# Two-layer relational graph convolution: sums by relation kept in a circle of 1024 nodes and projected once per block

## The chip, the cores and the metric

The kernel runs on one core of a Trainium2 chip. The metric is the device time of one execution in microseconds; the median of three runs before the change is 3974.79 us (3973.82 to 3981.2). A profile is one further execution, taken by the hardware profiler.

## The reference

Two layers of a relational graph convolution, then a residual and a layer normalisation. There are N = 12500 nodes of C = 128 features and E = 200000 edges, sorted by their target node `dst`. The type of an edge is the largest of ten of its attributes. Cut to what matters:

```python
def _rgcn_layer(x, src, dst, edge_type, w_rel, root, bias):
    seg = dst * NUM_REL + edge_type                       # NUM_REL = 10
    sums = segment_sum(x[src], seg, N * NUM_REL)
    cnt = segment_sum(ones, seg, N * NUM_REL)
    mean = (sums / maximum(cnt, 1)[:, None]).reshape(N, NUM_REL, -1)
    return einsum('nrd,rdo->no', mean, w_rel) + x @ root + bias

h = relu(_rgcn_layer(x, ..., w_rel1, root1, b1))
out = layernorm(x + _rgcn_layer(h, ..., w_rel2, root2, b2))
```

## The kernel before

**Tiles and groups.** The edges are cut into 1563 tiles of 128; one tile reaches over at most WN = 12 target nodes. Sixteen tiles are a group (97 full groups, then one of 8 and one of 3). Each layer runs over all groups in `layer` (L518).

**One group.** `gather` (L443) issues one indirect DMA per tile on POOL, which fetches the 128 source rows of the tile into `g`; three such buffers form a ring (RING = 3). `sums` (L454) builds on DVE one weighted one-hot matrix per tile, 128 edges by 120 columns (10 relations by 12 nodes), `oh` (L461), and TensorE multiplies `g` by it into `zp` in PSUM (L468). The first matmul in each group's order waits for all its gathers. An fp32 matmul shows as two records in the profile. ScalarE copies `zp` to `zs` (L482) in four pieces. `project` (L487) multiplies by the ten relation weights, two halves of 8 tiles, 40 records (L494), and ScalarE copies the result to `ms` (L500). `add` (L505) spreads the messages of the tiles over a window of 160 nodes with a further one-hot `at` (L465, L510), and DVE adds the window to the accumulator `acc`, 128 features by all nodes (L516), at an offset loaded into a register from the edges' first node (`bt`, L512, four offsets per load). Three groups are in flight: `sums` of k, `project` of k-1, `add` of k-2.

**Blocks.** When the groups that can touch a block of nodes are done (`done_after`, L76), the block is finished: 23 blocks of 512 nodes, then five of 128 and one of 84. `block_in` (L373) loads the block's own rows and transposes them on TensorE, `block_rows` (L391) adds the bias to the block's part of `acc` (L395), clears that part in layer 0 (L397), multiplies by `root` (L400) and brings the accumulator in by a product with the identity (L401). `hidden` (L408) applies ReLU and stores rows to `hD` in DRAM; `final` (L417) adds the residual, normalises on DVE and stores the output. Layer 1 gathers from `hD`, so its first gather waits for the last store of layer 0.

**What runs beside.** In layer 0 the types and counts of the edges are worked out for chunks of 128 tiles (`types`, `count`), spread over the groups as steps; they use DVE, PE and SP. Before the loop, `places` (L241) prepares the offsets, the first two chunks are typed and the first is counted. POOL does nothing in the loop but issue gathers. SP issues the loads and stores of blocks (L371).

**Order.** The order of instructions on each engine is chosen when the kernel is compiled, from dependences and the order of the program text; each engine then executes its queue in order. `tc.keep_in_program_order` and manual dependences pin a few of them. An instruction of DVE that uses a result of DVE waits for it. A general path for edges that do not fit the windows stands behind `tc.If(flag > 0)` (L738); it is not taken for this input.

Of the kernel before, what the change touches and what calls it, by code (L numbers as in the profile page):

```python
# [9 lines left out]
F32 = mybir.dt.float32  # L10
# [10 lines left out]
P = 128  # L21
# [3 lines left out]
WN = 12  # L25
# [4 lines left out]
HR = HT * WN  # L30
SW = 160
# [4 lines left out]
YB = 512  # L36
W = 128
# [6 lines left out]
def rgcn_resnorm_kernel(ctx: ExitStack, tc: tile.TileContext, x, src, dst, attr, w_rel1, root1, b1,  # L44
# [26 lines left out]
    NPAD = N + SW  # L71
# [15 lines left out]
    assert C == P and E % GT == 0 and 0 < HALF < P and NT % CT and groups[-1][1] > 1  # L87
# [5 lines left out]
    ps_f = ctx.enter_context(tc.tile_pool(name="ps_f", bufs=2, space=PSUM))  # L93
    ps_c = ctx.enter_context(tc.tile_pool(name="ps_c", bufs=1, space=PSUM))

    hD = dram.tile([N, C], F32, name="hD")
    KD = dram.tile([1, L + NT * P + L], F32, name="KD")
# [8 lines left out]
    zpool = fast.enter_context(tc.tile_pool(name="zpool", bufs=2))  # L106
    spool = fast.enter_context(tc.tile_pool(name="spool", bufs=3))
    ps_z = fast.enter_context(tc.tile_pool(name="ps_z", bufs=1, space=PSUM))
    ps_o = fast.enter_context(tc.tile_pool(name="ps_o", bufs=1, space=PSUM))
# [47 lines left out]
    def sources(c):  # L157
# [8 lines left out]

    columns = const.tile([P, SW], F32, name="columns")
    nc.gpsimd.iota(columns, pattern=[[1, SW]], base=0, channel_multiplier=0,
                   allow_small_or_imprecise_dtypes=True)
    iota = columns[:, :W]  # L170
    pads = const.tile([P, L + 1], I32, name="pads")
    nc.gpsimd.iota(pads, pattern=[[1, L + 1]], base=FAR, channel_multiplier=0)

    rank = const.tile([G, 2 * HR], F32, name="rank")
    nc.gpsimd.memset(rank, 1.0)
    nc.gpsimd.affine_select(rank, rank, pattern=[[1, 2 * HR]], compare_op=ALU.is_ge, fill=0.0, base=0,
                            channel_multiplier=-WN)
    nc.gpsimd.affine_select(rank, rank, pattern=[[-1, 2 * HR]], compare_op=ALU.is_ge, fill=0.0, base=WN - 1,
                            channel_multiplier=WN)
    lead = const.tile([G, 2 * HR], F32, name="lead")  # L180
    nc.gpsimd.memset(lead, 1.0)
    nc.gpsimd.affine_select(lead, lead, pattern=[[0, 2 * HR]], compare_op=ALU.is_equal, fill=0.0, base=0,
                            channel_multiplier=1)
    which = const.tile([G, 1], F32, name="which")
    nc.gpsimd.iota(which, pattern=[[0, 1]], base=0, channel_multiplier=WN, allow_small_or_imprecise_dtypes=True)
    row = const.tile([HR, 1], F32, name="row")
    nc.gpsimd.iota(row, pattern=[[0, 1]], base=0, channel_multiplier=1, allow_small_or_imprecise_dtypes=True)
    lane = const.tile([P, P], F32, name="lane")
    nc.gpsimd.iota(lane, pattern=[[1, P]], base=0, channel_multiplier=P,
                   allow_small_or_imprecise_dtypes=True)  # L190
    riota = const.tile([P, NREL], F32, name="riota")
# [3 lines left out]
    iotaP = bank[:, :SW]  # L195
    riotaP = bank[:, SW:SW + NREL]
# [13 lines left out]
    within = const.tile([HR, 1], F32, name="within")  # L210
    pw = ps_f.tile([P, YB], F32, name="pf")
    nc.tensor.matmul(pw[:HR, 0:1], rank[:, :HR], which, start=True, stop=True)
    nc.vector.tensor_tensor(within, row, pw[:HR, 0:1], op=ALU.subtract)
    nc.vector.tensor_tensor(rank, rank, lead, op=ALU.subtract)
    fl = const.tile([P, 1], F32, name="fl")
    nc.vector.memset(fl, 0.0)
    acc = const.tile([P, NPAD], F32, name="acc")
    negs = const.tile([1, L], F32, name="negs")
# [5 lines left out]
    bt = keep.tile([1, NG], I32, name="bt")  # L224
    b8_i = keep.tile([G, NG], I32, name="b8_i")
    full = NT // G
    nc.vector.memset(b8_i[:, full:], 0)
    nc.scalar.dma_start(bt[:, :full + 1], bass.AP(dst.tensor, dst.offset, [[1, 1], [G * P, full + 1]]))
    nc.scalar.dma_start(b8_i[:, :full], bass.AP(dst.tensor, dst.offset, [[P, G], [G * P, full]]))
    for k, (t, n) in list(enumerate(groups))[full:]:  # L230
        if k > full:
            nc.scalar.dma_start(bt[:, k:k + 1], bass.AP(dst.tensor, dst.offset + t * P, [[1, 1], [1, 1]]))
        m = n if t + n < NT else n - 1
        nc.scalar.dma_start(b8_i[:m, k:k + 1], bass.AP(dst.tensor, dst.offset + t * P, [[P, m], [1, 1]]))
    nc.scalar.dma_start(b8_i[m:n, NG - 1:], bass.AP(dst.tensor, dst.offset + E - P, [[1, 1], [1, 1]]))
    b8 = keep.tile([G, NG], F32, name="b8")
    place = keep.tile([HR, 2, NG], F32, name="place")
    wide = const.tile([P, 1], F32, name="wide")
    nc.vector.memset(wide, 0.0)

    def places():  # L241
        early(0, nc.vector.tensor_scalar(bt, bt, 0, N - 1, op0=ALU.max, op1=ALU.min))
        early(0, nc.vector.tensor_copy(b8, b8_i))
        pw = ps_f.tile([P, YB], F32, name="pf")
        for h in range(2):
            nc.tensor.matmul(pw[:HR, h * NG:(h + 1) * NG], rank[:, h * HR:(h + 1) * HR], b8, start=True, stop=True)
        nc.vector.tensor_scalar(place, pw[:HR, :2 * NG].rearrange("p (h g) -> p h g", h=2), within, None, op0=ALU.add)
        nc.vector.tensor_reduce(wide[:HR], place, axis=AX.XY, op=ALU.max)
# [123 lines left out]

    def block_in(k, l):  # L373

        n0, n, subs = block(k)
        last = "e" if k == NBLK - 1 else ""
        b = len(subs) if last else 4
        xb = fin.tile([P, b, C], F32, name="xb" + last)
        rows_dma(xb, x, k, False)
        fb = xb  # L380
        if l:
            fb = fin.tile([P, b, C], F32, name="hb" + last)
            rows_dma(fb, hD, k, False)
        pt = ps_f.tile([P, YB], F32, name="pf")
        for t, h in subs:
            nc.tensor.transpose(pt[:, t * P:t * P + h], fb[:h, t, :], ident[:h, :h])  # L386
        fT = fin.tile([P, b * P], F32, name="fT" + last)
        nc.scalar.activation(fT[:, :n], pt[:, :n], AF.Copy)  # L388
        return xb, fT

    def block_rows(fT, k, l):  # L391

        n0, n, subs = block(k)
        a = fin.tile([P, YB], F32, name="a")
        nc.vector.tensor_scalar(a[:, :n], acc[:, n0:n0 + n], bsb[l], None, op0=ALU.add)  # L395
        if l == 0:
            nc.vector.memset(acc[:, n0:n0 + n], 0.0)  # L397
        pr = ps_f.tile([P, 4, C], F32, name="pf")
        for t, h in subs:
            nc.tensor.matmul(pr[:h, t, :], fT[:, t * P:t * P + h], rsb[l], start=True, stop=False)  # L400
            nc.tensor.matmul(pr[:h, t, :], a[:, t * P:t * P + h], ident, start=False, stop=True)  # L401
        return pr
# [5 lines left out]
    def hidden(k, ready):  # L408

        xb, fT = ready  # L410
        pr = block_rows(fT, k, 0)
        hb = fin.tile([P, 4, C], F32, name="hb")
        for p, s in spans(k):
            nc.scalar.activation(hb[:p, s], pr[:p, s], AF.Relu)
        rows_dma(hb, hD, k, True)

    def final(k, ready):  # L417

        xb, fT = ready
        pr = block_rows(fT, k, 1)  # L420
# [30 lines left out]
    def halves(n):  # L451
        return [(h, min(HT, n - h * HT)) for h in range(-(-n // HT))]

    def sums(table, k, end):  # L454
# [8 lines left out]
        at = spool.tile([HR, 2, SW], F32, name="at")  # L463
        for h, _ in halves(n):
            nc.vector.tensor_scalar(at[:, h, :], iotaP[:HR], place[:, h, k:k + 1], None, op0=ALU.is_equal)  # L465
        zp = ps_z.tile([P, G // QB, YB], F32, name="zp")
        for j in range(n) if end else reversed(range(n)):
            m = nc.tensor.matmul(zp[:, j // QB, j % QB * KW:(j % QB + 1) * KW], g[:, j, :], oh[:, j, :],  # L468
                                 start=True, stop=True)
# [9 lines left out]
        zs = zpool.tile([P, NREL, G, WN], F32, name="zs")  # L479
        for b in range(-(-n // QB)):  # L480
            m = min(QB, n - b * QB)
            then("ACT", nc.scalar.activation(  # L482
                zs[:, :, b * QB:b * QB + m, :],
                zp[:, b, :m * KW].rearrange("c (j r n) -> c r j n", r=NREL, n=WN), AF.Copy))
        return k, zs, at

    def project(l, k, zs, at):  # L487

        n = groups[k][1]
        po = ps_o.tile([P, 2, C], F32, name="pp")  # L490
        ms = spool.tile([HR, 2, C], F32, name="ms")
        for h, m in halves(n):
            for r in range(NREL):
                nc.tensor.matmul(po[:m * WN, h], zs[:, r, h * HT:h * HT + m].rearrange("c j n -> c (j n)"),  # L494
                                 wsb[l][:, r, :], start=(r == 0), stop=(r == NREL - 1))
        if n % HT:
            for h, m in halves(n):
                nc.scalar.activation(ms[:m * WN, h], po[:m * WN, h], AF.Copy)
        else:
            nc.scalar.activation(ms[:, :n // HT], po[:HR, :n // HT], AF.Copy)  # L500
        return k, ms, at

    offs = []

    def add(k, ms, at):  # L505

# [266 lines left out]
```

## Time and profile before

| what | before |
|---|---|
| median of three runs | 3974.79 us |
| the profiled execution's own time | 4772.34 us |
| its span, first to last instruction | 4770.4 us |
| granted TensorE clock, mean | 0.739 |
| busy: PE / DVE / ACT / POOL | 2759.5 / 1511.5 / 527.0 / 2955.2 us |
| instructions: PE / DVE / ACT / POOL | 16162 / 4652 / 1136 / 3142 |
| DMA engines, mean busy share by slice | 0.1 to 0.4 |

The profiled execution took 798 us longer than the median of the runs. A line of the list of groups has line number, engine, operation, tiles, shapes and count, then busy time and the mean in ns of one, then the idle time of the engine just before, and what ended it; "issue" is time for which the profile shows no cause, and "remote" is a release that it could not trace. A line of the waits has engine, line and what it waited for, then the total, the number of waits and the longest. A line of the timeline has start, duration, engine, line, operation, tiles, shape and count, and in brackets the idle time before it. The chain of work that ended last is given by engine as:

```
another core or an unknown queue 34%; PE 33%; issue 21%; DVE 11%; ACT 1%; DMA 0%; DVEq 0%; ACTq 0%; SPq 0%
```

### The profile page before, as it was taken

Reading aid. Unit: us, or ns where it says so; the run is one execution under the profiler, and the core shown is the slowest. Engines: PE = TensorE matmul, PEld = TensorE weight load, DVE = VectorE, ACT = ScalarE, POOL = GpSimd, SP = SyncE. Lnnn points to the kernel's source line nnn. Section 1 sums busy time; section 2 is a strip of 40 time slices with the busy share of each in tenths; the row PEclk is TensorE's granted clock in tenths of the full one; section 3 lists DMA queues with packets and bytes.
Section 4 is the critical chain, followed back from the end, with each engine's and each line's share of the span. In section 5 each row is a group of like instructions: output and inputs, shape, how many; then the busy total and the mean of one; then the engine's idle time right before and its main releaser. Section 6 shows DMA issues by size and latency. Waiting matters only on the chain.

```text
span 4770.4 us, 43637 instructions
## 1 busy us (share of the span) xinstructions
PE 2759.5 (58%) x16162; PEld 2520.6 (53%) x16162; DVE 1511.5 (32%) x4652; ACT 527.0 (11%) x1136; POOL 2955.2 (62%) x3142
## 2 busy tenths in 40 slices
PE   2455556555655555666645555666655656565656
PEld 1455555555554545555544555555555555555556
DVE  5233333333333333333222222222222223222323
ACT  1011111111111101111110111111111111111111
POOL 5666665666656666666546666666666666666663
PEclk9677777777777777777776777777777777777778
DMA  4122122122221221212111211221222222222211
GB/s 141 44 79 74 50 74 74 50 75 62 61 77 47 75 62 51 57 48 52 46 49 46 54 52 51 53 56 51 52 56 53 52 52 58 51 52 52 58 52 40
DMA packets 180554, 279.00 MB, mean 58 GB/s; under 512 B 55623, under 2 KB 127190, under 8 KB 177206
## 3 DMA queue, kind: packets, MB, share of 16 engines
q0 software_dynamic: 100032, 205.07, 16.9%
q1 hardware_dynamic: 75428, 69.58, 4.6%
q8 instruction: 132, 2.16, 0.2%
q10 hardware_dynamic: 4872, 1.45, 0.1%
q14 instruction: 90, 0.74, 0.1%
HBM read 262.28 MB, written 13.60 MB: 58 GB/s over the span
## 4 chain that ended last, share of the span: by engine, by line
another core or an unknown queue 34%; PE 33%; issue 21%; DVE 11%; ACT 1%; DMA 0%; DVEq 0%; ACTq 0%; SPq 0%
PE pp L494 16%; PE zp L468 11%; DVE oh L461 7%; PE pp L510 2%; PE pf L401 1%; PE pf L400 1%; DVE at L465 1%; ACT zs L482 1%; DVE acc L516 1%; PE pf L343 0%; PE pf L345 0%; PE pf L386 0%; DVE o L436 0%; DVE st L429 0%
## 5 line engine op out<-in xcount | busy, mean ns | idle before, releaser
L445 POOL DMA_INDIRECT g<-in_x_dram,idxE x1563 | 1475.9, 944 | 911.2 <-issue 445.8
L445 POOL DMA_INDIRECT g<-hD,idxE x1563 | 1476.6, 945 | 865.3 <-issue 455.6
L494 PE MATMUL pp<-w,zs 128*96 128x128 f32 x7840 | 1358.2, 336 | 860.4 <-issue 722.1
L494 PEld LDWEIGHTS pp<-w,zs 128*96 128x96 f32 x7840 | 1232.0, 212 | 982.9 <-issue 834.6
L461 DVE TENSOR_SCALAR oh<-bank,keyE,wE 128x120 f32<-128x120 f32 x3126 | 1000.1, 400 | 644.6 <-remote 576.6
L468 PE MATMUL zp<-oh,g 128*128 128x120 f32 x6252 | 1033.5, 325 | 293.5 <-issue 259.9
L468 PEld LDWEIGHTS zp<-oh,g 128*128 128x128 f32 x6252 | 983.1, 240 | 314.0 <-issue 292.5
L482 ACT ACTIVATE zs<-zp 128x480 f32<-128x480 f32 (+1 forms) x782 | 382.9, 575 | 2167.7 <-remote 1912.9
L516 DVE TENSOR_TENSOR acc<-acc,pp 128x160 f32 x198 | 63.7, 322 | 1634.4 <-remote 1043.0
L510 PE MATMUL pp<-at,ms 96*128 96x160 f32 (+1 forms) x784 | 198.1, 386 | 591.1 <-issue 405.0
L510 PEld LDWEIGHTS pp<-at,ms 96*128 96x128 f32 (+1 forms) x784 | 142.5, 232 | 633.8 <-issue 437.1
L500 ACT ACTIVATE ms<-pp 96x256 f32<-96x256 f32 x196 | 74.1, 378 | 1241.3 <-remote 861.3
L341 DVE TENSOR_TENSOR eqb<-pf,kh 128x1344 bf16<-128x1344 f32 (+1 forms) x65 | 100.6, 1552 | 181.4 <-PE pf L345 82.3
L400 PE MATMUL pf<-root,fT 128*128 128x128 f32 x388 | 110.1, 379 | 79.0 <-issue 49.1
L401 PE MATMUL pf<-ident,a 128*128 128x128 f32 x392 | 114.0, 388 | 60.3 <-DVE a L395 22.0
L400 PEld LDWEIGHTS pf<-root,fT 128*128 128x128 f32 x388 | 87.0, 276 | 91.2 <-issue 55.8
L465 DVE TENSOR_SCALAR at<-bank,place 96x160 f32<-96x160 f32 x392 | 131.9, 376 | 0.0
L401 PEld LDWEIGHTS pf<-ident,a 128*128 128x128 f32 x392 | 90.7, 285 | 68.6 <-issue 24.6
L426 DVE TENSOR_TENSOR v<-pf,xb 128x512 f32<-128x512 f32 (+1 forms) x28 | 17.4, 620 | 243.2 <-remote 238.3
L348 DVE TENSOR_REDUCE wp<-pf 128x128 f32<-128x512 f32 (+1 forms) x13 | 9.0, 691 | 182.9 <-remote 175.5
L343 PE MATMUL pf<-eqb,identb 128*128 128x512 bf16 (+1 forms) x130 | 50.5, 388 | 17.9 <-DVE f L320 17.0
L388 ACT ACTIVATE fT<-pf 128x512 f32<-128x512 f32 (+1 forms) x56 | 30.2, 539 | 207.1 <-remote 151.3
(107 smaller groups left out, 483.0 us busy)
## 6 DMA issues: line engine op xcount, KB each, us to landing
m<-in_edge_attr_dram SPq DMA_DIRECT2D x24, 1344.0 KB
g<-in_x_dram,idxE POOLq DMA_INDIRECT x1563
g<-hD,idxE POOLq DMA_INDIRECT x1563
xb<-in_x_dram SPq DMA_DIRECT2D x46, 256.0 KB
hD<-hb SPq DMA_DIRECT2D x23, 256.0 KB
hb<-hD SPq DMA_DIRECT2D x23, 256.0 KB
out_dram<-o SPq DMA_DIRECT2D x23, 256.0 KB
w<-in_L_gnn_w_rel_dram ACTq DMA_DIRECT2D x2, 640.0 KB
```

Source lines behind the costliest of these rows:

```text
L341: nc.vector.tensor_tensor(eq[:p], kp[:p, None, :R].to_broadcast([p, DB, R]), ahead, op=ALU.is_equal)
L400: nc.tensor.matmul(pr[:h, t, :], fT[:, t * P:t * P + h], rsb[l], start=True, stop=False)
L401: nc.tensor.matmul(pr[:h, t, :], a[:, t * P:t * P + h], ident, start=False, stop=True)
L445: return g, [then("POOL", nc.gpsimd.indirect_dma_start(out=g[:, j, :], out_offset=None, in_=table, in_offset=bass.IndirectOffsetOnAxis(ap= ...
L461: then("DVE", nc.vector.tensor_scalar(oh[:, j, :], iotaP[:, :KW], keyE[:, t:t + 1], wE[:, t:t + 1], op0=ALU.is_equal, op1=ALU.mult))
L465: nc.vector.tensor_scalar(at[:, h, :], iotaP[:HR], place[:, h, k:k + 1], None, op0=ALU.is_equal)
L468: m = nc.tensor.matmul(zp[:, j // QB, j % QB * KW:(j % QB + 1) * KW], g[:, j, :], oh[:, j, :], start=True, stop=True)
L482: then("ACT", nc.scalar.activation(zs[:, :, b * QB:b * QB + m, :], zp[:, b, :m * KW].rearrange("c (j r n) -> c r j n", r=NREL, n=WN), AF.C ...
L494: nc.tensor.matmul(po[:m * WN, h], zs[:, r, h * HT:h * HT + m].rearrange("c j n -> c (j n)"), wsb[l][:, r, :], start=(r == 0), stop=(r == ...
L500: nc.scalar.activation(ms[:, :n // HT], po[:HR, :n // HT], AF.Copy)
L510: nc.tensor.matmul(pa, ms[:m * WN, h], at[:m * WN, h], start=(h == 0), stop=(h == len(parts) - 1))
L516: nc.vector.tensor_tensor(acc[:, s], acc[:, s], pa, op=ALU.add)
```

## The change

The sums by relation of each tile (`zp`, 128 features by 10 relations by 12 nodes) are no longer copied, projected and spread per group. DVE adds them, tile by tile, into ten accumulators of 1024 + 12 columns, `circle`, which lie in the memory of `acc`; a node's column is its number modulo 1024. The offset of each tile is loaded into a register, 16 per group. `zp` is now two PSUM buffers of half a group each, freed by these adds. When a block is done, `projected` multiplies its columns of the ten accumulators by the relation weights in one PSUM bank, 512 columns at a time with `root` as an eleventh term, and ScalarE clears the columns in two halves. The result has features on the partitions; ScalarE adds the bias (and ReLU in layer 0), and TensorE transposes it to rows. Layer 0 stores the block both as rows (`hD`) and transposed (`hT`), and layer 1 loads `hT` in place of `hD` for its `root` term. `places` clamps the first node of every tile to within 80 of an even spread. The core of the diff:

```diff
-SW = 160
+RN = 2 * YB
+RW = RN + WN
+OFF = 80
...
-    zpool = fast.enter_context(tc.tile_pool(name="zpool", bufs=2))
-    spool = fast.enter_context(tc.tile_pool(name="spool", bufs=3))
-    ps_z = fast.enter_context(tc.tile_pool(name="ps_z", bufs=1, space=PSUM))
-    ps_o = fast.enter_context(tc.tile_pool(name="ps_o", bufs=1, space=PSUM))
+    ps_z = fast.enter_context(tc.tile_pool(name="ps_z", bufs=2, space=PSUM))
...
+    even = keep.tile([1, NT], F32, name="even")
+    nc.gpsimd.iota(even, pattern=[[STEP, NT]], base=0, channel_multiplier=0, allow_small_or_imprecise_dtypes=True)
...
+    circle = acc[:, :NREL * RW].rearrange("p (r n) -> p r n", n=RW)
...
     def places():
-        early(0, nc.vector.tensor_scalar(bt, bt, 0, N - 1, op0=ALU.max, op1=ALU.min))
-        early(0, nc.vector.tensor_copy(b8, b8_i))
...
+        early(0, nc.vector.tensor_copy(bt, bt_i))
+        early(0, nc.vector.tensor_tensor(off, bt, even, op=ALU.subtract))
+        early(0, nc.vector.tensor_scalar(bt_i, off, float(OFF), -float(OFF), op0=ALU.min, op1=ALU.max))
+        early(0, nc.vector.tensor_tensor(bt_i, bt_i, even, op=ALU.add))
+        early(0, nc.vector.tensor_scalar(bt_i, bt_i, 0, N - 1, op0=ALU.max, op1=ALU.min))
+        early(0, nc.vector.tensor_scalar(bt_i, bt_i, RN - 1, None, op0=ALU.bitwise_and))
...
         if l:
-            fb = fin.tile([P, b, C], F32, name="hb" + last)
-            rows_dma(fb, hD, k, False)
+            then("SP", nc.sync.dma_start(fT[:, :n], hT[:, n0:n0 + n]))
+            return xb, fT
...
+    def projected(fT, k, l):
+        n0, n, subs = block(k)
+        po = ps_p.tile([P, YB], F32, name="pp")
+        nc.tensor.matmul(po[:, :n], rsb[l], fT[:, :n], start=True, stop=False)
+        o = n0 % RN
+        if not o and k:
+            nc.vector.tensor_tensor(circle[:, :, :WN], circle[:, :, :WN], circle[:, :, RN:], op=ALU.add)
+            nc.scalar.activation(circle[:, :, RN:], zero[:, None, :WN].to_broadcast([P, NREL, WN]), AF.Copy)
+        H = NREL // 2
+        for q in range(0, NREL, H):
+            for r in range(q, q + H):
+                nc.tensor.matmul(po[:, :n], wsb[l][:, r, :], circle[:, r, o:o + n], start=False, stop=(r == NREL - 1))
+            nc.scalar.activation(circle[:, q:q + H, o:o + n], zero[:, None, :n].to_broadcast([P, H, n]), AF.Copy)
+        return po
...
-    def block_rows(fT, k, l):
+    def block_rows(po, k, l):
         n0, n, subs = block(k)
         a = fin.tile([P, YB], F32, name="a")
-        nc.vector.tensor_scalar(a[:, :n], acc[:, n0:n0 + n], bsb[l], None, op0=ALU.add)
-        if l == 0:
-            nc.vector.memset(acc[:, n0:n0 + n], 0.0)
+        nc.scalar.activation(a[:, :n], po[:, :n], AF.Identity if l else AF.Relu, bias=bsb[l])
         pr = ps_f.tile([P, 4, C], F32, name="pf")
         for t, h in subs:
-            nc.tensor.matmul(pr[:h, t, :], fT[:, t * P:t * P + h], rsb[l], start=True, stop=False)
-            nc.tensor.matmul(pr[:h, t, :], a[:, t * P:t * P + h], ident, start=False, stop=True)
-        return pr
+            nc.tensor.transpose(pr[:h, t, :], a[:, t * P:t * P + h], ident)
+        return a, pr
...
     def hidden(k, ready, sums_of):
+        a, pr = block_rows(sums_of(fT, k, 0), k, 0)
+        then("SP", nc.sync.dma_start(hT[:, n0:n0 + n], a[:, :n]))
...
     def sums(table, k, end):
-        at = spool.tile([HR, 2, SW], F32, name="at")
...
-        zp = ps_z.tile([P, G // QB, YB], F32, name="zp")
+        zp = [ps_z.tile([P, HT // QB, YB], F32, name="zp") for _ in range(0, n, HT)]
...
-    def project(l, k, zs, at):
...
-    def add(k, ms, at):
...
+    def add(k, zp):
+        t0, n = groups[k]
+        lo, hi = bounds(t0, n)
+        lo, hi = (lo % RN, hi % RN) if lo // RN == hi // RN else (0, RN - 1)
+        offs = nc.values_load_multi_w_load_instructions(
+            bt_i[0:1, t0:t0 + n], engines=[DVE], min_val=lo, max_val=hi,
+            skip_runtime_bounds_check_because="clamped to these nodes on the chip")[1]
+        for j in range(n):
+            s = circle[:, :, ds(offs[j], WN)]
+            z = tile_sums(zp, j).rearrange("c (r n) -> c r n", n=WN)
+            nc.vector.tensor_tensor(s, s, z, op=ALU.add)
...
     def layer(table, l, finish, steps, flag_too=False):
...
         for k in range(NG):
             end = k >= NG - 2
-            if projected:
-                add_oldest()
             if end:
-                if held:
-                    project_oldest()
+                while held:
+                    add_oldest()
...
             held.append(sums(table, k, end))
-            if end and projected:
+            if len(held) > 1:
                 add_oldest()
-            if len(held) > 1:
-                project_oldest()
```

## The prediction

> **What bounds the kernel now.** I read the list of costliest groups first, then the waits, then stretches of the timeline, then single lines for durations. The groups:
>
> ```profile
> L445 POOL DMA_INDIRECT g<-in_x_dram,idxE x1563 | 1475.9, 944 | 911.2 <-issue 445.8
> L445 POOL DMA_INDIRECT g<-hD,idxE x1563 | 1476.6, 945 | 865.3 <-issue 455.6
> L494 PE MATMUL pp<-w,zs 128*96 128x128 f32 x7840 | 1358.2, 336 | 860.4 <-issue 722.1
> L461 DVE TENSOR_SCALAR oh<-bank,keyE,wE 128x120 f32<-128x120 f32 x3126 | 1000.1, 400 | 644.6 <-remote 576.6
> L516 DVE TENSOR_TENSOR acc<-acc,pp 128x160 f32 x198 | 63.7, 322 | 1634.4 <-remote 1043.0
> ```
>
> To see: 3126 gathers, one per tile, each 0.94 us of POOL. The timeline of POOL, over the end of a group of 16:
>
> ```profile
> 3046.45 0.94 POOL L445 DMA_INDIRECT g<-hD,idxE  x1 [0.30 <-issue]
> 3047.70 0.94 POOL L445 DMA_INDIRECT g<-hD,idxE  x1 [0.30 <-issue]
> 3048.95 0.94 POOL L445 DMA_INDIRECT g<-hD,idxE  x1 [0.30 <-issue]
> 3053.43 0.94 POOL L445 DMA_INDIRECT g<-hD,idxE  x1 [3.54 <-remote]
> ```
>
> Inside a group one gather starts 1.249 us after the last (0.944 busy, 0.30 of its own issue); at a group's border POOL waits 3.2 us more, for a buffer of the ring of three. The waits of POOL in total:
>
> ```profile
> POOL g L445 <- issue: 901.4, 2925, 5.1
> POOL g L445 <- remote: 456.6, 129, 8.1
> POOL g L445 <- PE zp L468: 383.2, 61, 28.5
> POOL g L445 <- DMA hD<-hb: 31.7, 1, 31.7
> ```
>
> So the profiled execution's span of 4770.4 us divides into 4 before the first gather, 3126 x 1.249 = 3904 of gathers, 28 of wait after the first three groups, 31 between the layers, 38 after the last gather, and some 765 at group borders. The plain runs take 3974.8. Taking off 2 us (the profiled execution's 4772.3 against its span), 4 and 3904 leaves 65 us for first wait, layer change, tail and all borders together, where the profiled execution has 97 for the first three alone. **In the plain runs, then, POOL hardly waits at borders: they are one queue of gathers.** Where do the 765 come from? TensorE's timeline:
>
> ```profile
> 612.70 0.60 PE L468 MATMUL zp<-oh,g 128*128 128x120 f32 x4
> 613.99 0.35 PE L468 MATMUL zp<-oh,g 128*128 128x120 f32 x1 [0.69 <-issue]
> 615.39 0.26 PE L468 MATMUL zp<-oh,g 128*128 128x120 f32 x1 [1.05 <-issue]
> 616.80 0.35 PE L468 MATMUL zp<-oh,g 128*128 128x120 f32 x1 [1.15 <-issue]
> ...
> 656.54 3.73 PE L468 MATMUL zp<-oh,g 128*128 128x120 f32 x32
> ```
>
> The same 32 records that take 3.73 us at 656 crawl at one per 1.4 us at 614, waiting for nothing. Such stretches of some 10 us recur about once a group. Without them PE has 14 us of work a group (32 records of L468 in 3.7 to 6.9, 40 of L494 in 4.5 to 6.3, the rest 2) in 20.0 of gathers. I take the crawl for an effect of recording, since the plain runs have no room for it.
>
> **The change, part by part.** Removed: per group 40 + 4 records on PE (L494, L510), four ACT copies (L482, 4 x 0.576), the ACT copy L500, two one-hots (L465, 2 x 0.29), one add (L516). By the argument above all of it lies under the gathers: worth 0 in plain runs, and still 0 if the PE cover shrinks, since it is itself what was covered.
>
> *Added: 16 adds a group on DVE.* Nearest row: L516, 322 ns for 160 columns from PSUM. L426 takes 692 for 512, so 1.05 ns a column and 280 ns for 120. Each add needs the one before; the dependent step L516 to L395 at 4743.92 to 4744.28 is 36 ns longer than L516. So 0.316 x 16 = 5.1 us. Bounds: 0.24 (the independent step after L516 at 3029.75) and 0.42 (280 + 36 + the register operation below unhidden, plus some dispatch); 3.8 to 6.7 a group. I take 5.1. The offsets:
>
> ```profile
> L516 DVEq FUSED_REGOPS  x198: 69/69/69, 95.8 to 4759.4; - x198
> L512 DVEq TENSOR_LOAD <-bt x50: 339/343/793, 95.1 to 4747.4; - x50
> ```
>
> One load brings four offsets in 343 ns; a load of one value (L546) takes 318. So 8 ns a value, and 16 in one load about 0.44 us; in four loads 1.4. The Trainium skill (Runtime: NRT & Kernel Launch, section Instruction fetch mechanics) prices such loads at about 200 ns a register; that is 3.2 us a group, 620 in all, and would speak against the change. Four for 343 ns contradicts it here, so I take 0.5. The 69 ns fit beside the add before.
>
> *DVE's total a group*: one-hots 16 x 0.31 = 5.0, adds and offsets 5.6, side work 1 to 2.5 (counting and types in layer 0, normalisation in layer 1): 12 to 13 of 20. It keeps up by sum. By the skill's price for loads, 15 to 16: still.
>
> *The new wait*: PSUM's two half-group buffers are freed by DVE's adds, no longer by ACT's copies. TensorE's group k+1, the projections and transposes queued behind it, wait for the adds of k. A serial cycle: 32 records 3.7 to 6.9 (take 5.5), adds and offsets 5.6, three hand-overs 1; 12 us. One-hots of k+2 run beside the matmuls of k+1. Cover is 20 us, with 20 more in the ring.
>
> *Per block of 512* (64 tiles, 4 groups), 22 PE records of 512 columns. Rows of 128 columns step at 0.112 or 0.213 us (612.25 to 612.47 is two records), so 0.45 to 0.85 each: 10 to 19, take 13. The second ACT clearing (5 x 512 columns; L388 takes 272 ns for 128, 597 for 512, so 2.3 us) follows. If adds behind the block must wait for both, a block costs 15 us of the cycle: 4 x 12 + 15 = 63 of 80. Gather k+3 needs only the matmuls of k, so one such jolt costs nothing.
>
> *Gathers beside a busier DVE.* The skill (SBUF — State Buffer, "DVE blocks DMA" trap) says an op in the two-port mode locks GpSimd out while descriptors are written. If the adds did so, 3126 x 0.28 = 875 us would be at stake. They have a PSUM input, like L461 and L516, and gathers beside L461's run of twelve at 3009.5 still start 1.25 apart (3010.71, 3011.96, 3013.20), so I take 0. Bounds 0 and 13: one gather in thirty longer by 0.12, as the one at 3009.35 beside L436, which reads and writes SBUF alone.
>
> *Start.* places() becomes six operations on one partition of 1563: by L395 (281 ns for 128, 501 for 512) 1.1 us for four and 1.8 for two, 8.0, less 1.7 removed: 6.3 on DVE at about 9 to 17 us. DVE is idle 5.4 us before 20.32 and 4.3 before 27.55 (edge attributes landing); that cover leaves 1 (0 to 6 if not). POOL's longer iota replaces six small ones.
>
> *Queues.* SP gets one store more per block (hT, 0.35 us issue) ahead of hD's and one load instead of hD's load; a block is 80 us. Only at the layer change is it on the path: its issue hides under the transpose and the ACT copy that precede hD's. 0 to 1.
>
> *Layer change and tail.* Before, a group's 40 records of L494 (4.5 us) stand between its neighbours; after, adds of 8 and 3 tiles (2.6 and 1 us), three small projections (22 records of 128 or fewer, 2.4 to 4.3 each) and a clearing, in a chain. Laid out from the last gather I get 15 to 21 us to the next layer against 18.5, 20 to 27 of tail against 24. Net 0, between -7 and +6 in all.
>
> Sum: 3974.8 + 1 + 1 + 0 = **3977 us**. Against the profiled execution itself: if the 765 vanish with half of PE's records, its time falls to about 4007; that gain is not in the plain runs.
>
> **The rivals.**
> 1. *Nothing measurable* (0.37, my forecast): POOL's queue stays the bound and start, layer change and tail nearly cancel, 3967 to 3983.
> 2. *DVE-PE cycle becomes the bound, slower* (0.35). In place: the loop of both layers, the adds of k before the matmuls of k+1. With 4 groups at TensorE's lower clock (6.9 + 1), side work unhidden (1.5) and a block's 19, 80 us are reached when an add with its offset costs (80 - 19 - 4 x 9.4) / 16 / 4 = 0.37. At 0.42, 3.5 us per four groups, 49 such fours: +170, 4150. If one-hots (5 us) fall into the cycle too: +5 a group at worst. Partly, with only some blocks stalling: 3990 to 4080. For it: DVE executes in order and waits on PE and DMA in layer 0. Against: the mid sum of 63, and the ring.
> 3. *Faster* (0.28): plain runs did wait at borders or carry a backlog into layer change and tail, which are lost with the PE work. The floor is 4 + 3904 + 2 + about 45 for the three fixed parts without backlog: 3955.
> 4. The fallback for skewed edges would add milliseconds; windows of 80 nodes around an even spread leave under 0.01 for it.
>
> **How the numbers follow.** 0.2% of 3975 is 8 us, about what a measurement here can tell from no change. Likeliest 3977. Below: 3950, the floor with a little profile error. Above: 4100, which takes in the partial cases of rival 2 and leaves its full size out. Within 0.2% alone the range would be 3967 to 3983.
>
> **What would show it.** Right: gathers still 1.249 apart, hardly any POOL wait at borders even in the profile, L494 and L510 gone, adds near 0.316 us apart and back to back, DVE about half busy. Rival 2: POOL waits for L468 at borders, PE for the adds. Rival 3: unchanged borders but earlier first gather of layer 2 and shorter tail. Wrong altogether if gathers slow down or if an add exceeds 0.4 us.

## The result and the profile after

The changed kernel takes 3994.91 us (median of 5 runs, 3991.56 to 3999.78) where the kernel before takes 3973.87 in the same series (3973.28 to 3981.2). The ratio is 1.0051, with a 95% interval of 1.004 to 1.0062: slower by half a per cent, 21 us. It lies in the range of the prediction, but not in its likeliest case, which was no measurable difference.

In some series of runs every kernel, the one before included, takes longer (the kernel before 4681 to 4758 us, without recording too), here called the other regime, and the first profile of the kernel before shows it, while the times of this result and the profile of the changed kernel do not.

The profiled execution of the changed kernel took 3999.78 us, with a span of 3998.0. The waits of POOL in it; the columns are total, number and longest, in us:

```profile
POOL g L450 <- issue: 939.6, 3082, 0.3
POOL g L450 <- DMA hD<-hb: 24.7, 1, 24.7
POOL g L450 <- PE zp L470: 18.0, 1, 18.0
```

The 456.6 us of "remote" and all but one of the 61 waits for L468 are not in it. That is not the work of the change: a later run of the kernel before without the other regime does not have them either. POOL waits twice for more than 1.3 us: 18 us after the third group, and 25 between the layers. Two of the groups:

```profile
L450 POOL DMA_INDIRECT g<-hD,idxE x1563 | 1478.5, 946 | 500.9 <-issue 471.3 <-DMA hD<-hb 24.7 <-DMA g<-hD,idxE 4.6
L493 DVE TENSOR_TENSOR acc<-acc,zp 128x120 f32 x3126 | 836.2, 268 | 1547.9 <-PE zp L470 1424.2 <-issue 70.7 <-ACT acc L386 47.6
```

The gathers are what they were (946 ns in the second layer, 949 in the first, one every 1.251 us). The 3126 adds take 268 ns each, and DVE waits 1424 us for the matmuls ahead of them, so it has time to spare. L494 and L510 have gone; PE has 8122 matmul records instead of 16162.

So the steady part is as predicted and the 21 us lie elsewhere. They can be found only where two profiles of the same regime are compared, which the experiments give.

### The profile page after: what moved, and what is told of

Same layout as the page of the kernel before. It is cut to its first block, busy times and chain, and to the rows that moved or that the text cites. A ratio compares the mean times of both kernels' runs of the same rounds, so it can differ in the third digit from the quotient of the medians.

```text
span 3998.0 us, 32286 instructions
## 1 busy us (share of the span) xinstructions
PE 1774.4 (44%) x8122; PEld 1417.2 (35%) x8122; DVE 1911.9 (48%) x7124; ACT 326.4 (8%) x325; POOL 2965.0 (74%) x3136
## 4 chain that ended last, share of the span: by engine, by line
POOL 64%; issue 25%; DMA 4%; PE 3%; DVE 2%; ACT 0%; DVEq 0%; POOLq 0%; ACTq 0%; SPq 0%
POOL g L450 64%; PE zp L470 2%; DMA g<-in_x_dram,idxE 2%; DMA g<-hD,idxE 1%; PE pp L385 1%; DVE acc L493 1%; DVE oh L466 1%; DMA m<-in_edge_attr_dram 0%; DVE bank L247 0%; DVE eq L249 0%; PE pf L404 0%; DMA bt_i<-in_dst_dram 0%; DMA root<-in_L_gnn_root_dram 0%; DVE bank L251 0%; DVE eq L250 0%
## 5 line engine op out<-in xcount | busy, mean ns | idle before, releaser
L470 PE MATMUL zp<-oh,g 128*128 128x120 f32 x6252 | 1163.1, 370 | 2056.7 <-DMA g<-hD,idxE 1004.8
L470 PEld LDWEIGHTS zp<-oh,g 128*128 128x128 f32 x6252 | 1125.0, 281 | 2163.0 <-issue 2130.4
L493 DVE TENSOR_TENSOR acc<-acc,zp 128x120 f32 x3126 | 836.2, 268 | 1547.9 <-PE zp L470 1424.2
L466 DVE TENSOR_SCALAR oh<-bank,keyE,wE 128x120 f32<-128x120 f32 x3126 | 1203.4, 393 | 14.2 <-PE zp L470 14.1
L385 PE MATMUL pp<-acc,w 128*128 128x512 f32 (+2 forms) x1160 | 438.4, 535 | 10.7 <-DVE acc L493 10.7
L386 ACT ACTIVATE acc<-zero 128x2560 f32<-128x2560 f32 (+2 forms) x116 | 231.9, 2000 | 1885.5 <-DVE acc L493 1334.0
L385 PEld LDWEIGHTS pp<-acc,w 128*128 128x128 f32 x1160 | 205.4, 198 | 209.7 <-issue 198.0
L377 PE MATMUL pp<-fT,root 128*128 128x512 f32 (+1 forms) x112 | 64.2, 659 | 17.4 <-ACT fT L370 17.4
L324 PE MATMUL pf<-eqb,identb 128*128 128x512 bf16 (+1 forms) x130 | 52.4, 403 | 36.5 <-DVE eqb L322 29.6
L404 PE MATMUL pf<-ident,a 128*128 128x128 f32 x196 | 43.0, 351 | 12.5 <-ACT a L401 12.5
L404 PEld LDWEIGHTS pf<-ident,a 128*128 128x128 f32 x196 | 34.6, 195 | 14.8 <-ACT a L401 14.8
L377 PEld LDWEIGHTS pp<-fT,root 128*128 128x128 f32 x112 | 20.8, 231 | 24.8 <-ACT fT L370 24.8
```

Source lines behind the costliest of these rows:

```text
L324: nc.tensor.matmul(pc[:p], identb[:p, :p], eq[:p, k:k + 4, L:], start=(d + k == 1), stop=False)
L377: nc.tensor.matmul(po[:, :n], rsb[l], fT[:, :n], start=True, stop=False)
L385: nc.tensor.matmul(po[:, :n], wsb[l][:, r, :], circle[:, r, o:o + n], start=False, stop=(r == NREL - 1))
L386: nc.scalar.activation(circle[:, q:q + H, o:o + n], zero[:, None, :n].to_broadcast([P, H, n]), AF.Copy)
L404: nc.tensor.transpose(pr[:h, t, :], a[:, t * P:t * P + h], ident)
L466: then("DVE", nc.vector.tensor_scalar(oh[:, j, :], iotaP[:, :KW], keyE[:, t:t + 1], wE[:, t:t + 1], op0=ALU.is_equal, op1=ALU.mult))
```

## The experiments

**Theory E**: the loss is made at the ends: at the start, at the change of layers and behind the last gather. **Theory C**: the gathers themselves became slower, since the after profile has them 1.251 us apart and the before profile 1.248 (means of the steps under 1.3 us), which over 3126 gathers is 7 us. **Theory S**: most of it is the start, by the operations of `places()`.

### Layer change and tail left out (two runs of each kernel)

The first edit lets the second layer gather from `x`, so that it waits for nothing and is computed on other data; the second leaves out the end of the last five blocks.

```diff
-    flag = layer(hD, 1, final, [(NG // 2, [1], flagged())], True)
+    flag = layer(x, 1, final, [(NG // 2, [1], flagged())], True)
```

> The kernel before, with layer 1 gathering from x instead of hD, so that no gather waits for the first layer's last rows (its second layer is computed on other data). Its time against the kernel before is what the layer change costs in plain runs, less what the ring itself still holds back. Theory E (the 21 us of the result were made at the ends and at the change: start 6, change 6, tail about 10, gathers themselves nearly unchanged): 3955, that is 18 to 20 us less. Theory C (the gathers themselves became slower, by 2 ns or more each, under a busier DVE): the same here, 18 to 20 less.

> The same edit in the changed kernel. Its profile shows 24.4 us of wait at the change. Theory E: about 3971, 24 us less than the changed kernel's 3995, so that the change cost 5 to 6 more than before. Theory C: the fall is 18 to 20 as in the kernel before and the two differ by 21 us still.

```diff
-                finish(done, ready if done == NBLK - 1 else block_in(done, l), projected)
+                if not l or done < NBLK - 5:
+                    finish(done, ready if done == NBLK - 1 else block_in(done, l), projected)
```

> The kernel before without the last five blocks' finish in layer 1 (root product, normalisation and store of some 600 nodes are left out). After the last gather only its group's one-hots, matmuls, projection and add remain. Theory E: 3962, 12 us less than the kernel before. Theory C: the same.

> The same edit in the changed kernel (projection, clearing, normalisation and store of the last five blocks are left out). Of the 36 us after the last gather the adds of the last groups remain, some 8. Theory E: 3967, 28 us less than the changed kernel, so that the two kernels without a tail differ by 5 to 8 only. Theory C: no more than 15 us less; the two differ by 18 or more still.

Measured: 4745.15, 4609.17, 4749.51 and 4607.06 us, in a series in which the kernel before took 4758.1. This is the other regime; against the result's 3974 these times tell nothing, and the four runs leave E and C undecided. Their traces still have ends. Where these were not left out, the kernel before waits 31.4 us at the change (b_notail) and has 36.5 behind the last gather (b_nowait); the changed one 38.9 and 49.3 (a_notail, a_nowait). So both ends are longer after the change here too, by 7.5 and 12.8 us.

They also show that the regime is not an effect of recording: the 30 plain runs of the kernel before in this series have it.

### A fourth gather buffer

```diff
-RING = 3
+RING = 4
```

> The changed kernel with four gather buffers instead of three; nothing else differs. Two regimes are open since the first four runs: in one (as in the result) the kernel before takes 3974 and POOL never waits at a group's border; in the other the kernel before takes 4758 even without recording, TensorE stands still for some 11 us in every group and POOL waits 3.2 us at every border. Theory E, first regime: the wait of 17.7 us that POOL's profile shows after the third group goes, 3995 becomes 3977. Theory C (slower gathers): the buffer is worth nothing by itself, since gathers only start earlier: 3995. In the second regime TensorE sets the pace, one more buffer shifts the wait by one group and is worth 20 us at most: about 4610.

Measured: 3976.26 us, ratio to the kernel before 1.0005 (0.9997 to 1.0014), in the regime of the result. The wait of 17.7 us after the third group is gone from the trace, and the time fell by 18.65 (3994.91 less 3976.26). So E has it right: that wait was wholly on the path. In this trace the gathers start 1.248 us apart, as before the change. Across all the recordings this step is either 1.248 or 1.251 and goes with the recording, not with the kernel (a_clear 1.248 and a_onehot 1.251, in one series; b_ring4_2 1.248 and b_ring4 1.251, one and the same kernel). **C falls**; the profiled execution of the changed kernel, with its 1.251, is also the slowest of its five runs, by 4.5 us.

### The kernel before once more, and three parts of the change one at a time

> The kernel before, unchanged, recorded once more: its first profile was of the regime in which TensorE stands still, so how its 64 us outside the gathers divide is not seen yet. Theory E (the difference of 21 us is made at the layer change and in the tail, with little at the start): wait after the third group 18 to 22, layer change 18 to 20, tail after the last gather 23 to 26. Theory S (it is made at the start, by the six operations on one partition): wait after the third group 8 to 12, change 24, tail 30.

```diff
-    loaded = set()
+    loaded = set(); placed = []
...
-        to_edges(wE, wp, c)
+        placed.append(to_edges(wE, wp, c))
...
-    places()
...
-    layer(x, 0, hidden, todo)
+    ahead[:] = placed; todo.insert(0, (0, [1], as_steps(lambda c: places(), 0))); layer(x, 0, hidden, todo)
```

> The changed kernel with the six operations of places() issued behind the first group's one-hots instead of at the start (they are still ahead of the first adds). Theory E: the edge types of the first chunk then begin some 6 us earlier, so does the first matmul, and the wait of 17.7 us after the third group shrinks by as much, if nothing else on the way to the first matmul takes its place: 3995 becomes 3989, at least 3993. Theory S: 3975 to 3980.

```diff
-            nc.scalar.activation(circle[:, q:q + H, o:o + n], zero[:, None, :n].to_broadcast([P, H, n]), AF.Copy)
+            if n0 + RN < NPAD: nc.scalar.activation(circle[:, q:q + H, o:o + n], zero[:, None, :n].to_broadcast([P, H, n]), AF.Copy)
...
     layer(x, 0, hidden, todo)
+    for a in range(0, NREL * RW, YB):
+        nc.scalar.activation(acc[:, a:min(a + YB, NREL * RW)], zero[:, :min(YB, NREL * RW - a)], AF.Copy)
```

> The changed kernel, where the blocks that lie in the last 1024 nodes are not cleared behind their projection; the accumulators are cleared once between the layers, behind the first layer's last block. Theory E: at the layer change and in the tail the adds of the last groups no longer wait for ScalarE's clearing (14.8, 9.8 and 4.8 us in the profile, most of it the projection itself): 2 to 3 us less at the change, 4 to 6 less in the tail, 3995 becomes 3987. If the projection sets the order anyway: 3994.

```diff
             if end:
-                while held:
-                    add_oldest()
...
-            held.append(sums(table, k, end))
+            s = sums(table, k, end)
+            next(s)
+            while end and held:
+                add_oldest()
+            held.append(next(s))
```

with `sums` yielding once behind its one-hots.

> The changed kernel, where the last two groups' gathers and one-hots are issued ahead of the adds and the blocks' ends that come before them, their matmuls behind as they were. Theory E: the one-hots of the group of eight no longer stand behind a block's normalisation (they began 11.7 us after the last gather): 4 us less in the tail, 0 to 2 less at the change, 3995 becomes 3990. If the chain of adds, projection and clearing is the longer one: 3994.

Measured: 4681.29, 4647.57, 4622.87 and 4635.2 us beside 4680.9 for the kernel before: the other regime again, so the times give no verdict on E or S. From the traces: leaving the clearing out shortens the change to 32.4 us, from 38.3 in a_onehot and 38.9 in a_notail; early one-hots bring the part behind the last gather to 46.9, from 48.4 in a_clear and 49.3 in a_nowait.

a_places is a miss with something in it. With `places()` out of the way the first chunk's keys are ready at 30.55 us instead of 39.18 (a_onehot), and no gather before 30 us is long any more. Instead, two gathers at 93 to 97 us are long (1.60 and 1.59 us), beside the same operations, which run at 87 to 96 us there. One of them:

```profile
95.06 1.59 POOL L450 DMA_INDIRECT g<-in_x_dram,idxE  x1 [0.31 <-issue]
```

But the first matmul comes later (87.4 against 80.9), because DVE itself crawls at 50 to 69 us. From the timeline of DVE there:

```profile
57.45 0.24 DVE L279 CAST d_f<-d_i 128x169 f32<-128x169 int32 x1
60.87 0.32 DVE L288 TENSOR_SCALAR key<-d_f 128x128 f32<-128x128 f32 x1 [3.18 <-issue]
```

Instructions that elsewhere follow each other within 0.3 us come 2 and 3 us apart, for nothing that the trace shows. It looks like the crawl that the prediction saw on TensorE, on another engine.

### The kernel before with four buffers, twice

The same edit of RING in the kernel before.

> The kernel before with four gather buffers instead of three. In the regime of the result, theory E: no wait after the third group, at the change 18 to 20 us, after the last gather 23 to 26; the time falls by the wait after the third group, 64 less change and tail, so 3974 becomes 3952 to 3956, and with four buffers the change costs 20 us or more. Theory S (the change lost time at the start): 3974 becomes 3963 or more, with change and tail of 27 and 33, hardly shorter than in the first profile. In the regime in which TensorE stands still: within 10 us of the kernel before.

> The kernel before with four gather buffers again, since its first run fell into the regime in which TensorE stands still. If this one falls into the regime of the result, theory E: no wait after the third group, at the change 18 to 20 us, after the last gather 23 to 26, and 3974 becomes 3952 to 3956. Theory S (the change lost time at the start): 3963 or more, with change and tail of 27 and 33. In the other regime: 10 to 20 us above the kernel before, as the first run of it, where TensorE sets the pace and one more buffer moves no wait.

The first run fell into the other regime: 4765.91 us, ratio 1.0026 (1.0014 to 1.0038), so there the fourth buffer buys nothing. The second ran in the regime of the result: 3959.37 us, ratio 0.9963 (0.9949 to 0.9977). The same kernel, waits of POOL, first in the other regime:

```profile
POOL g L445 <- remote: 445.9, 129, 3.7
POOL g L445 <- DMA hD<-hb: 41.0, 1, 41.0
```

and then in that of the result:

```profile
POOL g L445 <- issue: 943.8, 3097, 0.3
POOL g L445 <- DMA hD<-hb: 20.2, 1, 20.2
```

To see: no waits at borders at all, in a recorded run; the change costs 20 us, not 31 or 41. With the four-buffer kernel after the change (a_ring4; its first wait is that of the three-buffer one), this makes the budget that the result needs (us; the steps between gathers beyond 1.25, from the timelines of POOL, and for the first wait of the kernel before 3973.73 less 3959.37):

| part | before | after | difference |
|---|---|---|---|
| first gather starts | 4.3 | 4.5 | 0.2 |
| gathers held up, nearly all in the first 30 us | 0.6 | 3.8 | 3.2 |
| wait after the third group | 14.4 | 17.7 | 3.3 |
| wait at the layer change | 19.9 | 24.8 | 4.9 |
| behind the last gather | 26.6 | 36.1 | 9.5 |
| sum | | | 21.1 |

21.1 worked out, 21.0 measured: 6.7 at the start (the first three rows), 4.9 at the change, 9.5 in the tail. One entry is not from a trace: no profile of the three-buffer kernel before is of this regime, so its 14.4 is a difference of medians, and the interval of the ratio leaves 9 to 20 for it. That the sum comes out to 0.1 is therefore in part luck; the medians of the two four-buffer kernels differ by 16.9, where the rows without the first wait make 17.8. But change and tail are both from traces and make 14.4 of the 21.0, so that S falls however the rest divides: the start is a third. This is nearly the split with which E went into the first runs (6, 6, about 10); the narrower form that it had for b_again, with little at the start, does not hold. Of E's numbers for this run, change (18 to 20) and first wait (none) came, the tail was 0.6 above its 23 to 26, and the time 3 us above 3952 to 3956.

**The start.** DVE in a_ring4:

```profile
20.58 0.23 DVE L166 CAST s_f<-s_i 128x128 f32<-128x128 int32 x1 [4.11 <-DMA s_i<-in_src_dram]
20.73 1.77 DVE L227 TENSOR_TENSOR bt_i<-bt_i,even 1x1563 int32<-1x1563 int32 x1
22.42 1.77 DVE L568 TENSOR_TENSOR off<-off 1x1563 f32<-1x1563 f32 x1
24.12 0.95 DVE L228 TENSOR_SCALAR bt_i<-bt_i 1x1563 int32<-1x1563 int32 x1
25.11 0.96 DVE L229 TENSOR_SCALAR bt_i<-bt_i 1x1563 int32<-1x1563 int32 x1
26.84 0.82 DVE L249 TENSOR_TENSOR eq<-m,bank 128x640 f32<-128x640 f32 x1
```

and in b_ring4_2:

```profile
19.96 0.23 DVE L162 CAST s_f<-s_i 128x128 f32<-128x128 int32 x1 [5.12 <-DMA s_i<-in_src_dram]
20.10 0.81 DVE L268 TENSOR_TENSOR eq<-m,bank 128x640 f32<-128x640 f32 x1
```

The idle time that was to hide `places()` is there in both, 4 to 5 us before the cast of s_i. But four of the long operations stand behind that cast in DVE's order, one of them (L568, off times off) not even from `places()`: it belongs to the flag's test in the second layer and was scheduled up here. The comparison with the greatest type starts at 26.84 instead of 20.10, and the first matmul at 79.2 instead of 72.7. Beside and just behind these operations gathers get long, 1.73, 2.42, 1.39, 1.58 and 1.39 us; two of the five, POOL in a_ring4:

```profile
14.18 2.42 POOL L450 DMA_INDIRECT g<-in_x_dram,idxE  x1 [0.31 <-issue]
25.50 1.39 POOL L450 DMA_INDIRECT g<-in_x_dram,idxE  x1 [0.30 <-issue]
```

Five gathers that elsewhere take 0.945 each take 8.5 us together, 3.8 too long; b_ring4_2, without these operations, has none above 0.95 us behind its first one, and in a_places long gathers moved with the operations. That delay of the gathers takes as much off the wait after the third group, which is why a matmul 6.5 us later makes that wait only 3.3 longer.

**The tail**, behind a last gather that starts at 3936.34. From PE and DVE in a_ring4 (lines between these are left out):

```profile
3934.97 0.60 DVE L493 TENSOR_TENSOR acc<-acc,zp 128x120 f32 x2 [14.85 <-ACT acc L386]
3940.41 4.45 PE L385 MATMUL pp<-acc,w 128*128 128x128 f32 x20 [4.62 <-DVE acc L493]
3948.12 3.19 DVE L466 TENSOR_SCALAR oh<-bank,keyE,wE 128x120 f32<-128x120 f32 x10
3955.14 3.94 PE L385 MATMUL pp<-acc,w 128*128 128x128 f32 x20 [1.30 <-DVE acc L493]
3961.06 4.09 PE L385 MATMUL pp<-acc,w 128*128 128x84 f32 x20 [0.38 <-DVE acc L493]
```

It is one chain: adds of a group of 16 that had to wait for the clearing of the block before, its block's projection, normalisation, only then the one-hots of the last groups, matmuls, adds, projection, clearing, adds, projection. In b_ring4_2, where the last gather starts at 3928.04, three stations:

```profile
3932.56 2.58 DVE L461 TENSOR_SCALAR oh<-bank,keyE,wE 128x120 f32<-128x120 f32 x8
3938.74 2.13 PE L494 MATMUL pp<-w,zs 128*96 128x128 f32 x18
3946.57 0.32 DVE L516 TENSOR_TENSOR acc<-acc,pp 128x160 f32 x1 [1.24 <-PE pp L510]
```

One-hots 4.5 us behind the last gather instead of 11.8, and one add of 0.32 us for a group where there are now 16, 8 or 3.

**The granted clock at the ends.** The projections in this chain are slow for a reason of their own. Stretches of a_ring4, a projection at the layer change and two in the tail, then one of b_ring4_2; each line has the stretch, its length, busy time and count of PE, PEld, DVE, ACT and POOL (a count takes in records that only reach into the stretch), then the granted TensorE clock as a share of full speed, the DMA share and GB/s:

```profile
1974.94:1977.34 2.40, 2.39 (x22) 2.20 (x20) 1.67 (x1) 0.74 (x1) 0.00 (x0) 1.00 0.68 212
3940.41:3944.86 4.45, 4.45 (x20) 4.26 (x20) 0.27 (x1) 1.04 (x2) 0.00 (x0) 0.54 0.00 0
3955.14:3959.08 3.94, 3.94 (x20) 3.74 (x20) 0.00 (x0) 0.74 (x1) 0.00 (x0) 0.61 0.00 0
3938.74:3940.87 2.13, 2.13 (x22) 2.13 (x21) 1.28 (x5) 0.29 (x1) 0.00 (x0) 1.00 0.11 32
```

The same 20 records take 2.40 us at a granted clock of 1.00, and 4.45 and 3.94 at 0.54 and 0.61; length times clock is 2.40 each time. The kernel before has 1.00 at every projection of its tail. The third projection takes 4.09 at 0.57 and 2.46 at 1.00 (the one at 1979.61). So the three of the tail are 5.2 us longer than at full clock, of the 9.5. At the change it is 3.2 of the 4.9: a projection of 4.29 us at 0.56 in place of 2.40, and 16 records of L470 that take 3.28 at 0.58 and, in a_ends (the last run below) at 1.00, 1.95. All these steps hold up the next one in the chain, so an estimate from these durations is that 8.4 of the 14.4 us of both ends are the lower clock. No run here held the clock up to test it, and none shows what lowers it there. Over the whole run the mean granted clock is 0.700 in a_ring4 and 0.771 in b_ring4_2.

### Clearing and late one-hots taken out at both ends

Four buffers, a_clear's edit and a_onehot's edit together.

> The changed kernel with four gather buffers, the clearing of the last blocks moved between the layers, and the last two groups' one-hots ahead of the adds and ends of blocks before them (the three edits tried alone before). Theory E (what the change costs beyond the first wait is the chain adds, projection, clearing, adds at the two ends, and one-hots issued late): against the four-buffer kernel's 3976 the change falls from 24.8 to about 18 and the tail from 36 to 28 (8 us of late one-hots and clearing), 3962. If clearing and one-hots are covered by the projections, which are one chain of three: 3972 or more. In the regime in which TensorE stands still: about 4610, change near 32 and tail near 46.

Measured: 3971.68 us, ratio 0.9994 (0.9986 to 1.0003), in the regime of the result: 4.6 below the four-buffer kernel, where E expected 14 and its opposite 4. The change fell to 21.6 us, the part behind the last gather only to 35.2. Up to the last operation on DVE it is 29.1 us from the last gather's start against 31.9; the last store took 1.8 longer. The projections there (the last gather starts at 3931.47):

```profile
3937.63 4.64 PE L385 MATMUL pp<-acc,w 128*128 128x128 f32 x20 [7.74 <-DVE acc L493]
3947.91 3.62 PE L385 MATMUL pp<-acc,w 128*128 128x128 f32 x20 [2.11 <-DVE acc L493]
3953.37 4.56 PE L385 MATMUL pp<-acc,w 128*128 128x84 f32 x20 [0.21 <-DVE acc L493]
```

The clearing and the late one-hots are out of the chain, and three projections of 3.6 to 4.6 us with adds between them remain. Their granted clock is 0.50, 0.66 and 0.50; at 1.00 they would be 5.6 us shorter, by the durations above. So E was right on the place and too generous on these two causes: they are some 5 of the 14 us of both ends. That the rest is the projections in their order, at a low clock, is read from the timelines; no run took them away.

Among the kernels run, the fastest is the kernel before with four buffers, 3959.37; the changed kernel does not get there with the edits tried.

## Why the prediction was right or wrong

**The bound**: right. POOL's queue of gathers, 1.248 to 1.251 us each, sets the time before and after.

**The range**: the time lies in it in part by luck. With nothing for the gathers, the prediction's own upper ends for start, queues, layer change and tail (6, 1 and 6) reach 3988; the 3995 measured is covered because the range takes in the partial cases of rival 2, whose mechanism did not appear.

**The 765 us as an effect of recording**: wrong in its cause. Recorded runs without them exist (3955.9 us of span for b_ring4_2) and 30 plain runs with them. In every series on record all plain runs are of one regime; what sets it stays open. The conclusion drawn, that plain runs have no waits at borders, held for the runs of the result. The 4007 forecast for the profile after (measured 3999.78) came out for a reason other than the one given: that profile is of the result's regime. In the other regime, variants of the changed kernel (two of them with an end left out) took 0.968 to 0.994 of the kernel before; the changed kernel itself was not run there.

**Removed work worth 0**: right for the steady part; half of PE's records went and the gathers' step did not move. At the ends the granted clock is lower without this work; whether for want of it, no run shows.

**Adds and offsets**: an add and its step were right (0.31 us in a row, 0.316 predicted). The offsets were not. The one line of these loads:

```profile
L487 DVEq TENSOR_LOAD <-bt_i x198: 593/1100/1736, 80.9 to 3979.2; - x198
```

Sixteen values take 1.10 us, twice what was taken (0.5) and a third of what the Trainium skill (Runtime: NRT & Kernel Launch, section Instruction fetch mechanics) makes of them at 200 ns a register. The 8 ns a value came from a load of one beside one of four. Four, eight and sixteen values take 343, 593 and 1100 ns, some 63 ns a value; the count alone does not set it, since the last group's three take 758 and 866. DVE is busy for 48% of the span, as forecast, so the error costs nothing.

**The serial cycle of adds and matmuls**: right; after the third group POOL never waits at a border. Rival 2's mechanism did not appear, though slower is what came.

**Gathers beside a busier DVE**: for the adds 0 was right. But the rule that was weighed there, the Trainium skill's "DVE blocks DMA" trap (SBUF — State Buffer), was not applied to the new operations of `places()`, which read and write SBUF alone: 3.8 us on five gathers. The rule, which is stated for operations in the two-port mode, gives the right sign here, though no trace shows whether these run in that mode; the single row of 0.12 us a gather was far too small (0.76 on average).

**Start, +1 (0 to 6 if not covered)**: mis-sized, measured 6.7. The step that failed is "that cover leaves 1": the cover stood ahead of an instruction that waits, and 5.4 us of the work stood behind it. The six operations came to 7.4 us where 8.0 was taken, but L568 brought 1.8 more.

**Layer change and tail, "Net 0, between -7 and +6 in all"**: this is the step that failed most, measured +14.4. For the kernel before it was near (18.5 and 24 taken, 19.9 and 26.6 measured). After the change it said 15 to 21 and 20 to 27 and got 24.8 and 36.1. It counted the adds of 8 and 3 tiles and three projections at 2.4 to 4.3, but not the 16 adds that were still to do when the last gather was issued, nor the adds' wait for the clearing, nor that the last one-hots stand behind a block's normalisation. And it left the projections open between 2.4 and 4.3 each, without a look at which: the three of the tail took 4.45, 3.94 and 4.09, at a granted clock of 0.54 to 0.61.

**Rival 3's floor** of 3955 for a kernel without backlog was near, but it was the kernel before that came close to it, with a fourth buffer: 3959.

## What to carry to other kernels

When a queue hides everything in the middle, a change to the hidden work is paid at the ends: list what is left to do once the last transfer is issued, instruction by instruction in each engine's order, before calling it a draw, and look at the granted clock there: taking TensorE's work away from the middle went with a lower clock at the ends, where matmul time is on the path. Idle time covers new work only if the work stands ahead of the instruction that waits; look at which side of the wait the order puts it. And before two profiles are compared, compare each with its own plain runs: a profile that is 800 us above them may be of another regime, and its stretches of waiting then say nothing on the change.

## What the hardware showed unexpectedly

The granted TensorE clock stood at 0.50 to 0.66 during the projections of the changed kernel's tail and at 1.00 throughout those of the kernel before, and the length of a projection followed it in proportion (2.40 us at 1.00, 4.45 at 0.54).

In the other regime an engine's stream slows to one instruction every 0.7 us or a multiple for 10 to 20 us at a time (TensorE once a group, DVE in a_places), with nothing to wait for in the trace; the gathers' own step stays at 1.248 to 1.251. The kernel before loses 700 to 790 us to it. The mean granted clock of the kernel before is 0.74 to 0.75 there and 0.77 otherwise, far too little for that loss. It is not the chip: each of the three chips on record had both, and the same kernel (b_ring4) took 4765.91 in one series and 3959.37 in another.

A fourth buffer of the ring is worth 14.4 us before and 18.65 after; in the changed kernel it is all at one place, the border behind the first 48 gathers, and later POOL never waits for a buffer.
